# Graph attention and a graph convolution on one core: transposing x1's rows with VectorE and DMA in seven groups of eight, with Strassen products in three more places

## The chip, the cores and the metric

The kernel runs on one core of one Trainium2 chip, in float32 throughout. The metric is the device time of one execution in microseconds. Before the change the median of three runs was 2304.07 us (2303.71 to 2310.33).

## The reference

x is 4096 x 512, adj is 4096 x 4096. Two layers follow one another, each with a residual and a layer norm:

```python
q = x @ Wq.T + bq; k = x @ Wk.T + bk; v = x @ Wv.T + bv
a = q @ k.T / sqrt(512) + adj + adj
x1 = layernorm(x + softmax(a) @ v)
h = relu(adj @ (x1 @ W1) + b1)              # W1: 512 x 128
out = layernorm(x1 + adj @ (h @ W2) + b2)   # W2: 128 x 512
```

## The kernel before

**The arithmetic is rearranged.** With m = the product of Wk and Wq (`psm`, L856), the scores of a group of 512 query rows are x times u, where u = m applied to that group's x, scaled, plus a bias. So there is no q and no k. Behind the softmax, the kernel first forms the exponentials times x (called PX, tile `p`, L576), and only then multiplies the 512 rows of that sum (`ot`) by Wv (`rows_out`, L645, or `rows_out_fast`, L659). Then come the residual, the layer norm, and t = x1 W1 (`project`, `project2`), which layer 1 multiplies by adj.

**Groups and stages.** There are NG = 8 groups of W = 512 query rows. A group's scores (QK, `qk`, L429) are formed in 16 units of seven places; beside the QK products of group g, TensorE runs a paced list of other work: in the first group the u of later groups, afterwards PX of group g - 1, and in it the rows of group g - 2. After the last group's scores there are 16 more units in which PX of group 7 and the rows of group 6 run without QK beside them. Then layer 1 follows (`strassen`, L1049), with the rows of group 7 beside its first block.

**Strassen.** Most products are 2 x 2 block products done in seven multiplications (the Winograd form) rather than eight. `OPERANDS` names the left and right operand of each of the seven, `ORDER` is (1, 2, 6, 7, 5, 4, 3): products 1, 6, 5, 3 accumulate into one PSUM bank (X, or VX, PX) and 2, 7, 4 into others (Y, VY, PY). After each product the bank is read by VectorE (or ScalarE where a result begins) while the next product goes into the other bank; bank X is a single one, so product 1 of the next block of keys has to wait until product 3 has been read. T1 to T4 and S1 to S4 are sums of the blocks, made ahead by VectorE or GpSimd.

**What sets the order.** The schedule is written out by hand: an engine runs its instructions in the order in which the source emits them, and the SP queue issues its DMAs in that order too, each after what it has to wait for. `at(unit, place, f)` hangs a function on a place. `work[unit] = units, items` gives a list of (declared us, function) that is spread evenly over that many units (L1199 to L1219). `row_items` (L754) makes the items of a group's rows; `between`, called `w(n)` in it, takes n products out of the PX list, so that w(4) puts four PX products between two row items.

**The parts that the change touches.**

- Startup (L793 to L879): the four transposed weight halves are loaded, Wq and Wk are transposed by TensorE (`psw`, L848), m is formed (L856), and u of group 0 by plain products (`u_products`, L254, L262); u of group 1 also plainly, in the first three units (`work[0]`). u of groups 2 to 7 is formed by Strassen's products (`u_fast`, L194, L234) in the 13 units after (`work[3]`).
- u's buffers: `new_uo` (L165) has a ring of three for B11 and B12 and one buffer (`uo`, 1280 KB over all partitions) for the other five operands. `store_u` writes them to DRAM (`u_d`), and the group reads them back as `ut` when its turn comes. The large store is issued after product 3.
- Rows: `FAST_V = range(NG - 2)`: rows of groups 0 to 5 by Strassen's products, of 6 and 7 by the plain `rows_out`.
- Projection: `project` (L736) transposes a normalised row tile (128 rows x 512) by four TensorE transposes against the identity into one bank (`x1ps`, L740), ScalarE copies it to `x1t` (L742), and `project2` (L745) multiplies it by W1 (`tps`, L749), after which VectorE copies the 128 x 128 result to `t_sb`. `xr` holds a group's x1 rows; `rowp`, where `xr` and `x1t` lie, has one buffer for each name.
- `add_b2` (L729) adds b2 to a row tile on GpSimd and stores it for the end (`x1_d`).
- `sum_t` (L945): the S sums of t for layer 1, on GpSimd.

Of the kernel before, what the change touches and what calls it, by code (L numbers as in the profile page):

```python
# [11 lines left out]
F32 = mybir.dt.float32  # L12
# [12 lines left out]
def tile_graph_attention_then_gcn(  # L25
# [59 lines left out]
    NCK = N // CW  # L85
    PER = W // P
# [19 lines left out]
    c_d = [dram.tile([1, W], F32, name=f"c_d{g}") for g in range(NG)]  # L106
    u_d = [dram.tile([P, 7, 2, HW], F32, name=f"u_d{g}") for g in range(NG)]
# [46 lines left out]
    FAST_V = range(NG - 2)  # L154
# [10 lines left out]
    def new_uo(b, what):  # L165

        u = UO.setdefault(b, {})
        if what in (B11, B12):
            u[what] = uop.tile([P, 2, HW], F32, tag="b1", name=f"b1_{b}_{what}", bufs=3)
        else:  # L170
            u["all"] = uop.tile([P, 5, 2, HW], F32, tag="ut", name=f"uo{b}")
            u.update({k: u["all"][:, k - 1] for k in range(1, 6)})

    def store_u(b, what):
        if what in (B11, T4):
            nc.gpsimd.dma_start(u_d[b][:, what], UO[b][what])
        else:
            nc.gpsimd.dma_start(u_d[b][:, 1:6], UO[b]["all"])

    def m_sums():  # L180
# [6 lines left out]
        for out_, a, b_ in ((T1, T3, B11), (T2, B22, T1), (T4, B21, T2)):  # L187
            nc.gpsimd.tensor_tensor(MV[out_], MV[a], MV[b_], ALU.subtract)

    def m_t3():  # L190

        nc.vector.tensor_tensor(MV[T3], MV[B22], MV[T3], ALU.subtract)

    def u_fast(b):  # L194
# [4 lines left out]
        def read(k):  # L199
            ps = X["X" if k in (1, 6, 5, 3) else "Y"].rearrange("p (o i) -> p o i", o=2)  # L200
            if k == 1:
                new_uo(b, B11)
            if k == 6:
                new_uo(b, B12)
            if k == 7:
                new_uo(b, "all")
# [10 lines left out]
            if k == 4:  # L217
                for out_, a, b_ in ((T1, B12, B11), (T2, B22, T1), (T3, B22, B12)):
                    nc.gpsimd.tensor_tensor(u[out_], u[a], u[b_], ALU.subtract)
                store_u(b, B11)  # L220
            if k == 3:
                store_u(b, "all")
                owing.append(lambda: last(b))

        def last(b):
            nc.vector.tensor_tensor(UO[b][T4], UO[b][B21], UO[b][T2], ALU.subtract)
            store_u(b, T4)
# [25 lines left out]

    def u_products(b):  # L254

        ps = {}

        def one(o, c):
            def go():
                if c == 0:  # L260
                    ps[o] = bank("o", f"psu{b}_{o}", 4)
                nc.tensor.matmul(  # L262
                    ps[o], m_t[:, c, ts(o, P)], XTS[b][:, c, :], start=c == 0, stop=c == ND - 1
                )
                if c == ND - 1:
                    if o == 0:
                        if b:
                            for what in (B11, B12, "all"):
                                new_uo(b, what)
                        else:  # L270
                            for k in ORDER:
                                new_operand(0, k)
                    pair = (B11, B12) if o < 2 else (B21, B22)
                    for h in range(2):
                        nc.scalar.activation(
                            (UO[b][pair[h]] if b else UT[0, pair[h]])[:, o % 2, :],
                            ps[o][:, ts(h, HW)],
                            AF.Identity,
                            bias=ub_t[:, o : o + 1],
                            scale=HALF_SCALE,  # L280
                        )
                    if o == ND - 1:
                        if b:
                            combine_u(nc.gpsimd, UO[b])
                            for what in (B11, "all", T4):
                                store_u(b, what)
                        else:
# [1109 lines left out]
```

## Time and profile before

| | |
|---|---|
| median of three runs | 2304.07 us (2303.71 to 2310.33) |
| the profiled execution's own time | 2308.84 us |
| its span, first to last instruction | 2307.1 us |
| granted TensorE clock, mean | 0.998 |
| DMA moved | 525.14 MB, mean 228 GB/s |
| transposes of rows (L740) | 128, on TensorE |
| copies of them (L742) | 32 on ScalarE, 587 ns each |
| plain products of u (L262) | 64 pieces, in groups 0 and 1 |
| plain products of rows (L651) | 64 pieces, in groups 6 and 7 |

The page lists an engine's busy time, the chain of work that ended last, the groups of instructions with the idle time before them, and the DMAs with the time from issue to landing. PE is TensorE, PEld its weight loads, DVE is VectorE, ACT is ScalarE, POOL is GpSimd, SP issues DMAs. A float32 matmul of the source stands in the trace as two pieces, a transpose as one. Matmuls are pipelined, so what one costs is the distance from its start to that of its neighbour, not its own duration.

### The profile page before, as it was taken

What the parts mean: (1) busy time and instruction counts of PE and PEld (TensorE: products, weight loads), DVE (VectorE), ACT (ScalarE), POOL (GpSimd) and SP (SyncE); (2) the same over time, 40 slices, a digit from 0 to 9 for tenths busy, and PEclk for the clock granted to TensorE, in tenths of its full rate; (3) what the DMA queues carried; (4) which work ended last, traced back from release to release, by engine and by line L of the source; (5) the groups of instructions that cost most, each with busy time, mean ns of one, the idle gap of its engine ahead of it and who ended that gap; (6) DMA issues with size and microseconds to landing.
All of it is one profiled execution on the core that took longest, in us unless ns stands there. A gap on an engine that the chain in (4) does not pass through costs nothing.

```text
span 2307.1 us, 28475 instructions
## 1 busy us (share of the span) xinstructions
PE 2276.3 (99%) x10672; PEld 1750.6 (76%) x10672; DVE 1617.0 (70%) x2276; ACT 399.8 (17%) x438; POOL 1018.7 (44%) x1009
## 2 busy tenths in 40 slices
PE   9999999999999999999999999999999999999998
PEld 5888788888888888888888888888876743333456
DVE  4676776687667756765776687568657877888864
ACT  2212211131122112111311121122102000000012
POOL 3565654185327424731653274237429830001043
PEclk9999999999999999999999999999999999999999
DMA  6999878667857684777578586947754468899996
GB/s 177 273 284 309 233 215 230 193 174 215 246 135 218 189 246 114 215 213 215 151 221 232 145 218 193 259 117 210 196 191 155 155 237 321 332 347 375 352 383 218
DMA packets 282711, 525.14 MB, mean 228 GB/s; under 512 B 23184, under 2 KB 130448, under 8 KB 281680
## 3 DMA queue, kind: packets, MB, share of 16 engines
q1 hardware_dynamic: 229040, 406.12, 52.3%
q0 software_dynamic: 43296, 105.39, 20.7%
q10 hardware_dynamic: 10240, 11.82, 1.7%
q8 instruction: 85, 1.39, 0.2%
q14 instruction: 50, 0.41, 0.0%
HBM read 475.27 MB, written 46.41 MB: 226 GB/s over the span
## 4 chain that ended last, share of the span: by engine, by line
PE 92%; DVE 4%; POOL 2%; DMA 1%; issue 1%; ACT 0%; SPq 0%; POOLq 0%; DVEq 0%; ACTq 0%
PE p L576 32%; PE X L436 18%; PE b L1041 15%; PE Y L436 14%; PE v L703 3%; PE acce L1342 2%; PE psu L234 2%; PE ops L1296 1%; PE tps L749 1%; PE psu L262 1%; PE x L651 1%; PE x1ps L740 1%; DVE s L449 1%; PE psm L856 1%; DMA u_d<-uo 1%
## 5 line engine op out<-in xcount | busy, mean ns | idle before, releaser
L576 PE MATMUL p<-s,xn 128*128 128x256 f32 x3584 | 895.6, 380 | 7.0 <-DVE s L531 2.6
L576 PEld LDWEIGHTS p<-s,xn 128*128 128x128 f32 x3584 | 677.1, 190 | 111.0 <-DVE s L531 5.6
L436 PE MATMUL X<-ut,sa 128*128 128x256 f32 x1984 | 513.4, 381 | 1.7 <-DVE s L449 1.7
L492 POOL TENSOR_TENSOR lacc<-lacc,s 128x512 f32<-128x512 f32 x240 | 344.1, 1434 | 203.2 <-ACT s L483 192.3
L436 PEld LDWEIGHTS X<-ut,sa 128*128 128x128 f32 x1984 | 370.1, 190 | 64.2 <-DVE s L449 15.3
L449 DVE TENSOR_TENSOR s<-X,s 128x512 f32<-128x512 f32 x256 | 176.3, 689 | 278.6 <-PE X L436 278.2
L436 PE MATMUL Y<-ut,sa 128*128 128x256 f32 x1408 | 361.6, 380 | 0.2 <-DVE s L449 0.2
L436 PEld LDWEIGHTS Y<-ut,sa 128*128 128x128 f32 x1408 | 266.8, 190 | 37.7 <-issue 1.4
L483 ACT ACTIVATE s<-s 128x1024 f32<-128x1024 f32 x128 | 135.3, 1057 | 790.3 <-DVE s L479 790.3
L458 DVE TENSOR_TENSOR macc<-macc,s 128x512 f32<-128x512 f32 x240 | 258.1, 1075 | 1.2
L449 DVE TENSOR_TENSOR s<-Y,s 128x512 f32<-128x512 f32 x192 | 131.9, 687 | 157.0 <-PE Y L436 155.7
L479 DVE TENSOR_TENSOR s<-s,mb 128x512 f32<-128x512 f32 x256 | 231.2, 913 | 2.4 <-ACT mb L399 2.4
L385 POOL DMA_DIRECT2D s<-in_adjT_dram x64 | 84.4, 1318 | 256.7 <-ACT s L380 255.9
L549 DVE TENSOR_TENSOR ot<-p,ot 128x512 f32<-128x512 f32 x248 | 168.9, 681 | 31.4 <-PE p L576 31.2
L1008 DVE TENSOR_TENSOR tt<-ck 128x1024 f32<-128x1024 f32 x112 | 138.4, 1270 | 38.7 <-PE b L1041 33.6
L1041 PE MATMUL b<-tt,st 128*64 128x512 f32 (+1 forms) x768 | 156.0, 541 | 0.0
L380 ACT COPY s<-cb 128x2048 f32<-128x2048 f32 x64 | 121.0, 1890 | 48.1 <-PE p L576 39.8
L519 POOL TENSOR_TENSOR s<-s 128x256 f32<-128x256 f32 x128 | 124.6, 974 | 0.6
L1041 PEld LDWEIGHTS b<-tt,st 128*64 128x64 f32 x768 | 53.9, 137 | 87.8 <-issue 79.9
L526 DVE TENSOR_TENSOR s<-s 128x512 f32<-128x512 f32 x128 | 114.3, 914 | 0.0
L520 POOL TENSOR_TENSOR s<-s 128x256 f32<-128x256 f32 x128 | 107.8, 842 | 10.0
L489 POOL TENSOR_TENSOR lacc<-s 128x512 f32<-128x512 f32 x8 | 10.6, 1321 | 197.9 <-ACT s L483 197.9
(186 smaller groups left out, 2112.6 us busy)
## 6 DMA issues: line engine op xcount, KB each, us to landing
ck<-in_adjT_dram SPq DMA_DIRECT2D x128, 1024.0 KB, 7.4
s<-in_adjT_dram POOLq DMA_DIRECT2D x64, 1024.0 KB, 11.5
sa<-s_d SPq DMA_DIRECT2D x224, 256.0 KB, 5.7
xn<-in_x_dram SPq DMA_DIRECT2D x192, 256.0 KB, 4.3
xn<-xs_d SPq DMA_DIRECT2D x96, 512.0 KB, 5.7
sa<-in_xT_dram SPq DMA_DIRECT2D x168, 256.0 KB, 4.7
xn<-xs_d SPq DMA_DIRECT2D x64, 256.0 KB, 3.9
ut<-u_d SPq DMA_DIRECT2D x49, 256.0 KB, 7.2
```

Source lines behind the costliest of these rows:

```text
L380: nc.scalar.copy(s, CB[g].unsqueeze(1).to_broadcast([P, 4, W]))
L436: nc.tensor.matmul(T["X" if k in (1, 6, 5, 3) else "Y"][:, ts(j, HW)], SA[g, d, a][:, c, j, :], UT[g, b][:, c, :], start=k in (1, 2, 7) an ...
L449: nc.vector.tensor_tensor(ck, ps, ck, ALU.add)
L458: nc.vector.tensor_tensor(MACC[g], MACC[g], ck[:, h, :], ALU.max)
L479: nc.vector.tensor_tensor(ck, ck, MB[g], ALU.subtract)
L483: nc.scalar.activation(ck, ck, AF.Exp, scale=2.0)
L492: nc.gpsimd.tensor_tensor(LACC[g], LACC[g], ck[:, h, :], ALU.add)
L519: nc.gpsimd.tensor_tensor(b12, b12, b11, ALU.subtract)
L549: nc.vector.tensor_tensor(to, ps, to, ALU.add)
L576: nc.tensor.matmul(T["PX" if k in (1, 6, 5, 3) else "PY"][:, ts(f, HW)], XN[n][:, q - a, ts(f, P)], quarters(g, q)[{1: 0, 2: 2, 6: 1, 7: 0 ...
L1008: nc.vector.tensor_tensor(t[:, :2], v[:, :, 1], v[:, 0], ALU.subtract)
L1041: nc.tensor.matmul(BK[n][k][ts(half, HH)], lhs, right(u, i, half, b), start=q == 0, stop=q == NP - 1,)
```

## The change

1. **Transposes of rows.** For groups 0 to 6, `project` is replaced by three steps. `turn_blocks` transposes each 32 x 32 block of the row tile in place of its position with one VectorE instruction, into `x1t`. `store_blocks` writes x1t to DRAM (`xt_d`) with four DMAs of 32 partitions each, issued on SP, so that the blocks land transposed also among each other: each DMA writes 512 runs of 32 elements. `load_blocks` reads the tile back, 128 runs of 2 KB, over the row tile in `xr`, and `project2` multiplies from there. Group 7 keeps `project`.
2. **The order of row items** for those groups is new: b2, turn, store and load of the four row tiles, with w(...) between. `by = 3` (three PX products for one in the last group) is gone, with numbers of its own for group 6.
3. **FAST_V** is `range(NG - 1)`: group 6's rows by Strassen's products too, their operand sums on GpSimd for that group.
4. **u.** `u_products` is gone; u of group 0 by `u_fast` at the startup, its last sums on VectorE, and u of groups 1 to 7 in 15 units from unit 1. B21 joins B11 and B12 in a ring that has four buffers; the single buffer holds the other four operands, and is stored after product 4, not after product 3. B21's store is issued on ScalarE's queue.
5. **Startup.** m's products are taken in another order, beginning before all of Wk has been transposed; m's operand sums are made there, two on VectorE and two on GpSimd, and the first sums of x follow m's second row.
6. **sum_t:** the second half, layer 1's sums over t tiles 16 to 27, is issued three units later.

```diff
+    xt_d = {
+        (g, r): dram.tile([P, ND, P], F32, name=f"xt_d{g}_{r}")
+        for g in FAST_V
+        for r in range(PER)
+    }
...
-    FAST_V = range(NG - 2)
+    FAST_V = range(NG - 1)
...
-        if what in (B11, B12):
-            u[what] = uop.tile([P, 2, HW], F32, tag="b1", name=f"b1_{b}_{what}", bufs=3)
+        if what in (B11, B12, B21):
+            u[what] = uop.tile([P, 2, HW], F32, tag="b1", name=f"b1_{b}_{what}", bufs=4)
         else:
-            u["all"] = uop.tile([P, 5, 2, HW], F32, tag="ut", name=f"uo{b}")
+            u["all"] = uop.tile([P, 4, 2, HW], F32, tag="ut", name=f"uo{b}")
...
     def store_u(b, what):
+        if what == B21:
+            nc.scalar.dma_start(u_d[b][:, what], UO[b][what])
...
             if k == 4:
...
+                if b:
+                    store_u(b, B11)
+                    store_u(b, "all")
             if k == 3:
-                store_u(b, "all")
+                if b:
+                    store_u(b, B21)
...
+        sum_ = (nc.gpsimd if g == NG - 2 else nc.vector).tensor_tensor
...
+    def turn_blocks(g, r):
+        T["x1t", g, r] = rowp.tile([P, ND, P], F32, tag="x1t", name=f"x1t{g}_{r}")
+        nc.vector.transpose(T["x1t", g, r].rearrange("p c i -> p (c i)"), XR[g][:, r, :])
+
+    def store_blocks(g, r):
+        x1t = T.pop(("x1t", g, r))
+        to = xt_d[g, r].rearrange("(b i) c (a j) -> a i c b j", i=32, j=32)
+        for a in range(4):
+            nc.sync.dma_start(
+                to[a], x1t[ts(a, 32)].rearrange("i c (b j) -> i c b j", j=32)
+            )
+
+    def load_blocks(g, r):
+        T["x1t", g, r] = XR[g][:, r, :].rearrange("p (c i) -> p c i", i=P)
+        nc.sync.dma_start(T["x1t", g, r], xt_d[g, r])
...
+            a, b, c, d, e, f = (1, 8, 2, 6, 5, 11) if g < NG - 2 else (3, 14, 4, 10, 6, 22)
             return [
                 *(item(0.86, rows_out_fast, g, k, j) for k in ORDER for j in range(2)),
-                *w(1), item(0, rows_last, g), *norm(2), *norm(3), *w(2), *pro(2), *w(2), *pro(3),
-                *w(1), *norm(0), *w(1), *pro2(2), *norm(1), *w(2), *pro(0), *w(2), *pro2(3), *w(2),
-                *pro(1), *w(2), *pro2(0), *w(4), *pro2(1), *w(2), *b2(2), *w(4), *b2(3), *w(4), *b2(0),
-                *w(4), *b2(1),
+                *w(a), item(0, rows_last, g), *norm(2), *norm(3), *w(b), *norm(0), *w(c), *norm(1),
+                *w(d // 2), *b2(2), *w(d - d // 2), *turn(2), *w(e), *store(2), *b2(3), *w(f),
+                *turn(3), *load(2), *w(e), *store(3), *b2(0), *w(f), *turn(0), *load(3), *pro2(2),
+                *w(e), *store(0), *b2(1), *w(f), *turn(1), *load(0), *pro2(3), *w(e), *store(1),
+                *w(f), *load(1), *pro2(0), *w(f), *pro2(1),
             ]
...
-    work[0] = 3, [(0.86, f) for f in u_products(1)]
-    work[3] = 13, [(0.86, f) for g in range(2, NG) for f in u_fast(g)] + [(0, lambda: owing.pop()())] * 2
-    at(1, 0, m_sums)
-    at(3, 0, m_t3)
+    work[1] = 15, [(0.86, f) for g in range(1, NG) for f in u_fast(g)] + [(0, lambda: owing.pop()())] * 2
...
-            by = 3 if g == NG - 1 else 1
-            items = row_items(g - 1, lambda n: [px.pop() for _ in range(n * by)])
+            items = row_items(g - 1, lambda n: [px.pop() for _ in range(n)])
...
-    at(last_unit - 5, 0, lambda: [sum_t(0, 0, 8), sum_t(8, 8, 14)])
+    at(last_unit - 5, 0, sum_t, 0, 0, 8)
+    at(last_unit - 2, 0, sum_t, 8, 8, 14)
```

## The prediction

> **What bounds the kernel now.** I read the page's busy line first, then its chain, then the groups by form, the chain in order of time, the waits of TensorE, VectorE and the DMA issues.
>
> ```profile
> PE 2276.3 (99%) x10672; PEld 1750.6 (76%) x10672; DVE 1617.0 (70%) x2276; ACT 399.8 (17%) x438; POOL 1018.7 (44%) x1009
> ...
> PE p L576 32%; PE X L436 18%; PE b L1041 15%; PE Y L436 14%; PE v L703 3%; PE acce L1342 2%; PE psu L234 2%; PE ops L1296 1%; PE tps L749 1%; PE psu L262 1%; PE x L651 1%; PE x1ps L740 1%; DVE s L449 1%; PE psm L856 1%; DMA u_d<-uo 1%
> ```
>
> TensorE is busy 99% and nearly the whole chain is matmuls: one microsecond of matmul work less is one microsecond less, unless a wait takes its place. The chain in order of time gives what a piece costs when pieces follow one another (the mean of a group holds the pipeline's depth, so it is too long):
>
> ```profile
> 25.51 3.43 PE psu L262 x8
> 29.38 10.30 PE psu L262 x24
> ...
> 656.18 1.73 PE v L703 x8
> ...
> 870.58 1.73 PE v L703 x8
> ```
>
> A 512-column piece takes 3.43/8 = 0.429 us, a 256-column piece 1.73/8 = 0.216. (Each matmul of the source is two pieces, a transpose one.) The same product returns after 870.58 - 656.18 = 214.4 us: a row group's period. The timeline of TensorE shows a transpose between neighbours:
>
> ```profile
> 893.83 0.66 PE L740 MATMUL x1ps<-ident,xr 128*128 128x128 f32 x4 [0.37 <-ACT xr L639]
> 894.32 0.60 PE L576 MATMUL p<-s,xn 128*128 128x256 f32 x2
> ...
> 896.05 0.60 PE L740 MATMUL x1ps<-ident,xr 128*128 128x128 f32 x4
> 896.49 1.03 PE L436 MATMUL X<-ut,sa 128*128 128x256 f32 x4
> ```
>
> Four transposes hold it 896.49 - 896.05 = 0.44 us, and the first four of a group also wait 0.37 us for the normalised row. TensorE's waits:
>
> ```profile
> PE X L436 <- DVE s L449: 4.1, 5, 1.0
> ...
> PE x1ps L740 <- ACT xr L639: 2.3, 6, 0.4
> PE psu L234 <- ACT uo L211: 1.9, 1, 1.9
> PE x1ps L740 <- ACT x1t L742: 1.5, 1, 1.5
> ...
> PE tps L749 <- ACT x1t L742: 0.7, 1, 0.7
> ```
>
> **The change, part by part.** The profiled execution took 2308.84 us, its span 2307.1.
>
> *Transposes.* Seven groups of four row tiles lose their four PE transposes: 28 x 0.44 = **-12.3 us**. In the changed program's instruction order 16 transposes of rows are left, those of the last group. Their waits go as well: 2.3 for the rows, and 1.5 + 0.7 in the stage where the seventh group's rows are made: **-4.5**. What is late next is project2, which now needs the loaded tile. Its load is issued 16 paced items ahead of it; a list of 113.7 us of declared work (224 products of 0.43, rows 12.0, projections 5.4) is spread over 214.4 us, so an item of 0.43 takes 0.81 us, and 16 take 13 us. The 256 KB loads of xn and sa land in 4 to 6 us, so this stays covered.
>
> *Strassen in three more places.* u of groups 0 and 1 and the rows of group 6 take 28 matmuls of 256 columns in place of 16 of 512: 32 x 0.429 = 13.73 against 56 x 0.216 = 12.10, three times: **-4.9**. Group 0's u is not interleaved with anything; each accumulating bank is read (two ACT pieces of 0.47, or one DVE piece of 0.68) while the other bank takes 1.73 us of product, so I add no wait. The startup's other matmuls are the same ones in another order (the order shows as many of each); DVE reaches c_sb at 22.8 us before, and the new place of the transposes that need it is at about 23.5, so 0.
>
> *u's buffers.* The one big wait of the u stage is 1.9 us for a 1280 KB store of uo that holds the single buffer. Now four of its five parts are stored, a product earlier, and the fifth goes to the ring of four: **-1.9**.
>
> *Group 6's operand sums on POOL.* Three sums precede the sixth product. POOL adds 128x512 in 1.27 to 1.43 us; beginning about 1 us after the last PX read they end at 4.9 to 5.3, and the third product of the order wants the last of them after two products, 3.46 us: **+1.6**. The wait of 0.9 of x (L651) for xr goes with the plain form: **-0.9**.
>
> *VectorE's blocks.* 28 block transposes of 128x512 are not in this trace. Bounds: a copy of that shape 0.69 us, the strided subtraction of L328 1.34 us. I take 0.69 (one input, one output, as the copy), 19 us in all. VectorE's own waits show the cover:
>
> ```profile
> DVE s L449 <- PE X L436: 278.2, 187, 3.2
> DVE s L449 <- PE Y L436: 155.7, 113, 3.2
> ```
>
> It waits for TensorE 434 us, 1.5 at a time, and the bank it empties is needed again one product later (1.73 of its own, 2.0 of the interleaved list), so it may be about 2.5 us late before PE waits. Only where product 3 is followed by product 1 in the same bank is there no slack; the 4.1 us above are those. 28 transposes of 0.69, one product in seven: at most 28 x 0.69 / 7 = 2.8, **+1.5** taken; without cover it is 19 to 37.
>
> *The trip through DRAM, the real unknown.* x1t has one buffer, so the next tile's block transpose (VectorE, in order) waits until all four stores of the tile before have landed, and behind it queue the reads of X, Y and p that TensorE waits for. SP's load of the tile waits for the same landings, and behind it queue the sa and xn loads; those are issued some five products ahead, 19 us, and need 6, so SP can stand about 13 us and VectorE gives way first. Stores and transpose are 11 items apart, 8.9 us (22 items of 0.43, 9.5 us, in group 6). Each store writes 512 runs of 128 bytes. The nearest rows:
>
> ```profile
> c_d<-c_sb ACTq DMA_DIRECT2D x7, 2.0 KB, 9.8
> ...
> s_d<-sa SPq DMA_DIRECT2D x32, 256.0 KB, 7.8
> x_d<-xb POOLq DMA_DIRECT2D x32, 256.0 KB, 4.0
> ```
>
> c_d's store is 512 runs too, of 4 bytes; s_d's are four stores in a row on SP. Low end: 256 KB lands as x_d, 4.0. High end: the four follow one another at c_d's pace, 39. I take 9, between s_d (four issues) and c_d (short runs): as long as the window, so VectorE is held little and its 2.5 us of slack take most of it. 21 such waits (three a group): **+2** for the queueing of some behind large loads.
>
> The Trainium skill, page "DMA: Bandwidth & Descriptors", section "Rules for kernel authors", speaks against this step: a transpose by rearranged access pattern in a plain DMA is put at 19 times the hardware's, and its "Specifications" ask for 512 bytes or more a run. c_d's 9.8 us for 2 KB agrees in direction; no run here shows 128 bytes. An estimate from the page alone: 256 KB at its 435 GB/s is 0.6 us, 19 times that 11.4, on top of s_d's 7.8 gives 19 us, 10 past the window, and 21 x (10 - 2.5) = +160 us. I weigh it less, because runs of 32 elements are not single elements.
>
> *Moves.* The later second sum_t and the spread row items in the last two stages, and the ACT copies saved, hide behind other work: 0.
>
> Sum: -12.3 - 4.5 - 4.9 - 1.9 + 1.6 - 0.9 + 1.5 + 2 = -19.4. On the profiled execution's own time: 2308.8 - 19.4 = 2289.4. The median of the runs is 4.8 under that execution (2304.07), so **2284.6**; I say 2285.
>
> **Rivals.**
> (a) *The stores hold VectorE.* One mechanism: four stores land late, the next block transpose stands at the head of VectorE, X and Y are not read. Each microsecond past 8.9 + 2.5 = 11.4 costs 21. Without the +2 the gain is 21.4, so it turns the sign at 11.4 + 1.0 = 12.4 us. At 15 us: 21 x 3.6 - 21.4 = +54, 2358; at c_d's pace (39 us) 21 x 27.6 = 580 more, 2860. For it: c_d's short runs. Against: the x_d and s_d rows with far more bytes.
> (b) *Half the gain goes in the last stage.* From 1700 to 1860 us TensorE already waits for VectorE and POOL (L531, L526, L549: 5.2 us) and the change adds seven reads of 0.68 for four, and four block transposes. At 5 to 10 us more: 2290 to 2295.
> (c) *That stage gets better.* Row items stood between 96 products, now 165, so VectorE's bursts are thinner; if the 5.2 us and as much of their smaller kin go: 2275.
> (d) *Waits of 1 us at each of the 21 places* beyond the +2: no change, 2304.
>
> **Chances.** Forecast 0.56, (b) 0.15, (c) 0.12, (d) 0.04, (a) 0.13. About 0.3%, 7 us, is what a measurement here tells from no change. Faster: 0.56 + 0.15 + 0.12 = 0.83; same 0.04; slower 0.13. The range reaches from 2266 (case (c), low ends of the unknowns) to 2303, leaving out (a), some of (d) and little below.
>
> **What would show it.** Right: no x1ps in groups 0 to 6, PE busy down by about 18, sixteen plain row matmuls left of 32, block transposes near 0.7 us, stores landing in under 11 us, no new TensorE wait over 5 us. Wrong: a line "DVE x1t <- DMA" of tens of microseconds, with waits of X and Y on s behind it; loads of sa or xn late on SP; or block transposes well over 1.3 us.

## The result, and the profile after

The changed kernel takes **2325.2 us** (median, 2323.64 to 2329.25), the kernel before in the same comparison 2305.07: **ratio 1.0086, 95% interval 1.0073 to 1.0099**. It is slower by about 20 us, where 2285 was forecast. The profiled execution's span grew from 2307.1 to 2327.4 us.

The busy line and the chain of the page after:

```profile
PE 2267.3 (97%) x10632; PEld 1753.7 (75%) x10632; DVE 1636.9 (70%) x2315; ACT 386.3 (17%) x414; POOL 1024.6 (44%) x1007
...
PE p L550 30%; PE X L410 18%; PE b L1054 15%; PE Y L410 13%; PE v L679 3%; PE psu L252 3%; PE acce L1356 2%; DVE s L453 2%; PE ops L1310 1%; PE tps L743 1%; DVE s L500 1%; DVE s L505 1%; DVE s L423 1%; DMA t_sb<-in_x_dram 1%; DVE macc L432 1%
```

TensorE has 40 pieces fewer, as counted out (112 transposes less, three times 56 for 32 more), and is busy 9 us less, but its share fell from 99% to 97%, and five lines of VectorE stand in the chain in place of one. TensorE's longest sums of waits in the kernel after (total, times, longest, us):

```profile
PE p L550 <- DVE ot L523: 21.1, 14, 1.7
PE p L550 <- DVE s L500: 8.7, 14, 1.7
PE X L410 <- DVE s L423: 6.7, 4, 4.7
PE p L550 <- DVE s L505: 4.1, 7, 0.6
```

L550 is the PX product (L576 before), L523 its read, L500 and L505 the sums of exponentials that are its operands. The same three waits before:

```profile
PE p L576 <- DVE s L531: 2.6, 2, 1.7
PE p L576 <- DVE s L526: 2.3, 5, 0.7
PE p L576 <- DVE ot L549: 1.4, 2, 0.9
```

What was feared did not come: the block transposes and their stores, in the kernel after:

```profile
L725 DVE STREAM_TRANSPOSE x1t<-xr x28: 694/699/703, 477.8 to 1816.5; 128x512 f32<-128x512 f32 x28
```

```profile
DMA to landing us min/median/max: 2.2/4.9/11.7
```

0.70 us each, never lengthened, and VectorE has no wait on x1t's stores at all.

**Where the time came.** By the first matmul of each stage: the startup is 1.4 us shorter, the stages of groups 0 and 1 (the u work) together 1.7 longer, the six stages in which rows of groups 0 to 5 are made **21.0 longer**, the stage after the last scores 1.4 shorter, layer 1 the same 368.7, the tail 0.4 longer: +20.3. The six are alike, so one is enough. In the stage of group 3's scores I mark three points: the first PX product, the 57th (the end of the stretch in which the first 56 products stand beside the rows' other work; the *short stretch* below) and the last (the *long stretch*). Busy time by stretch, before; the columns are window, its length, then busy us and instructions of PE, PEld, DVE, ACT and POOL, clock, DMA share and GB/s:

```profile
676.70:732.80 56.10, 55.67 (x277) 48.09 (x277) 45.74 (x63) 18.32 (x21) 46.89 (x47) 1.00 0.69 189
732.80:867.20 134.40, 134.40 (x625) 117.33 (x624) 85.81 (x120) 19.35 (x16) 48.95 (x42) 1.00 0.80 223
```

The same two stretches after:

```profile
681.00:734.40 53.40, 48.47 (x222) 40.52 (x221) 46.52 (x58) 13.07 (x15) 48.02 (x46) 1.00 0.81 207
734.40:874.70 140.30, 140.30 (x665) 123.13 (x664) 87.64 (x129) 22.20 (x18) 49.35 (x43) 1.00 0.84 225
```

The reader is to see two things. The short stretch lost 55 TensorE pieces and is only 2.7 us shorter; TensorE now stands idle in it for 5 us, with VectorE busy 46.5 and GpSimd 48.0 of 53.4 us. The long stretch gained 40 pieces and is 5.9 us longer, TensorE busy without a gap in both kernels. Two queries of the same windows tell which pieces went over. Those of the scores (L436), before:

```profile
676.70:732.80 56.10, 30.02 (x117) 1.00 0.69 189
732.80:867.20 134.40, 72.44 (x281) 1.00 0.80 223
```

and of the scores (L410) after:

```profile
681.00:734.40 53.40, 25.90 (x101) 1.00 0.81 207
734.40:874.70 140.30, 76.44 (x297) 1.00 0.84 225
```

Sixteen score pieces changed sides, and the projections of three tiles too (32 pieces of `tps` stood in the short stretch before, 8 stand there after, 24 in the long one).

### The profile page after: what moved, and what is told of

The parts are those of the page before. It is cut to its first block, busy times and chain, and to the rows that moved or that the text cites. A ratio compares the mean times of both kernels' runs of the same rounds, so it can differ in the third digit from the quotient of the medians.

```text
span 2327.4 us, 28683 instructions
## 1 busy us (share of the span) xinstructions
PE 2267.3 (97%) x10632; PEld 1753.7 (75%) x10632; DVE 1636.9 (70%) x2315; ACT 386.3 (17%) x414; POOL 1024.6 (44%) x1007
## 4 chain that ended last, share of the span: by engine, by line
PE 88%; DVE 7%; DMA 3%; issue 1%; SPq 0%; POOL 0%; ACT 0%; POOLq 0%; DVEq 0%
PE p L550 30%; PE X L410 18%; PE b L1054 15%; PE Y L410 13%; PE v L679 3%; PE psu L252 3%; PE acce L1356 2%; DVE s L453 2%; PE ops L1310 1%; PE tps L743 1%; DVE s L500 1%; DVE s L505 1%; DVE s L423 1%; DMA t_sb<-in_x_dram 1%; DVE macc L432 1%
## 5 line engine op out<-in xcount | busy, mean ns | idle before, releaser
L550 PE MATMUL p<-s,xn 128*128 128x256 f32 x3584 | 899.1, 381 | 35.6 <-DVE ot L523 21.1
L550 PEld LDWEIGHTS p<-s,xn 128*128 128x128 f32 x3584 | 677.2, 190 | 148.4 <-DVE ot L523 26.7
L410 PE MATMUL X<-ut,sa 128*128 128x256 f32 x1984 | 514.3, 382 | 5.8 <-DVE s L423 5.8
L410 PEld LDWEIGHTS X<-ut,sa 128*128 128x128 f32 x1984 | 372.2, 190 | 68.3 <-DVE s L423 20.3
L410 PE MATMUL Y<-ut,sa 128*128 128x256 f32 x1408 | 360.6, 379 | 2.4 <-DMA sa<-in_xT_dram 2.4
L410 PEld LDWEIGHTS Y<-ut,sa 128*128 128x128 f32 x1408 | 266.0, 190 | 38.1 <-DVE s L453 2.7
L453 DVE TENSOR_TENSOR s<-s,mb 128x512 f32<-128x512 f32 x256 | 237.0, 932 | 0.4 <-ACT mb L373 0.4
L432 DVE TENSOR_TENSOR macc<-macc,s 128x512 f32<-128x512 f32 x240 | 227.8, 949 | 1.4
L523 DVE TENSOR_TENSOR ot<-p,ot 128x512 f32<-128x512 f32 x248 | 168.9, 681 | 27.1 <-PE p L550 27.0
L1021 DVE TENSOR_TENSOR tt<-ck 128x1024 f32<-128x1024 f32 x112 | 138.9, 1275 | 38.7 <-PE b L1054 34.1
L500 DVE TENSOR_TENSOR s<-s 128x512 f32<-128x512 f32 x128 | 126.3, 1007 | 0.0
L493 POOL TENSOR_TENSOR s<-s 128x256 f32<-128x256 f32 x128 | 123.3, 963 | 0.6
L494 POOL TENSOR_TENSOR s<-s 128x256 f32<-128x256 f32 x128 | 118.1, 923 | 10.1
L463 POOL TENSOR_TENSOR lacc<-s 128x512 f32<-128x512 f32 x8 | 10.6, 1322 | 199.0 <-ACT s L457 199.0
## 6 DMA issues: line engine op xcount, KB each, us to landing
s<-in_adjT_dram POOLq DMA_DIRECT2D x64, 1024.0 KB, 11.7
```

What stands on the lines that cost most here:

```text
L410: nc.tensor.matmul(T["X" if k in (1, 6, 5, 3) else "Y"][:, ts(j, HW)], SA[g, d, a][:, c, j, :], UT[g, b][:, c, :], start=k in (1, 2, 7) an ...
L432: nc.vector.tensor_tensor(MACC[g], MACC[g], ck[:, h, :], ALU.max)
L453: nc.vector.tensor_tensor(ck, ck, MB[g], ALU.subtract)
L493: nc.gpsimd.tensor_tensor(b12, b12, b11, ALU.subtract)
L500: nc.vector.tensor_tensor(b, b, t2, ALU.subtract)
L523: nc.vector.tensor_tensor(to, ps, to, ALU.add)
```

## The experiments

Times are medians; ratios are against the kernel before, run beside them, with their 95% intervals. Stretch lengths are those of a middle group.

**1. Which part of the change?** The rows of groups 0 to 5 alone put back, all else changed:

```diff
+            if g < NG - 2:
+                return [
...
+                    *w(1), item(0, rows_last, g), *norm(2), *norm(3), *w(2), *pro(2), *w(2), *pro(3),
...
             a, b, c, d, e, f = (1, 8, 2, 6, 5, 11) if g < NG - 2 else (3, 14, 4, 10, 6, 22)
```

> The changed kernel with the rows of groups 0 to 5 made as before the change (TensorE transposes, old order of row items); group 6, u and the startup stay changed. After the change each of the six row stages is 3.3 to 3.9 us longer than before, the startup 1.4 and u 0.5 shorter, the last stage 1.5 shorter. All theories put the loss into the rows of groups 0 to 5, so all expect about 2300 us (2297 to 2304). Above 2312 would mean that the loss lies elsewhere.

Measured 2304.38, ratio 0.9991 (0.998 to 1.0002). So the loss lies in those rows. The rest of the change together is worth about 2 us, by the interval between 4.6 us gained and 0.5 lost.

**2. The trip.** No stores and no loads:

```diff
-        for a in range(4):
-            nc.sync.dma_start(
-                to[a], x1t[ts(a, 32)].rearrange("i c (b j) -> i c b j", j=32)
-            )
...
-        nc.sync.dma_start(T["x1t", g, r], xt_d[g, r])
```

> The changed kernel without the stores to DRAM and the loads back (it leaves out the trip, so project2 multiplies the untransposed tile); block transposes, b2 and the order of items stay. Trip theory (short runs hold VectorE, SP or the DMA engines): the six stages lose their 5.5 us each, about 2292. Beside theory (b2 on GpSimd and block transposes on VectorE fall into the stretch in which VectorE has the short PX blocks): 2318 to 2326. Pace theory (the PX list runs earlier against the shifts because no projection holds it back): 2318 to 2326.

Measured 2324.36, 1.0077 (1.0062 to 1.0092): the trip costs nothing here.

**3. VectorE's transposes.** Left out, the stores reading the row tile:

```diff
-        T["x1t", g, r] = rowp.tile([P, ND, P], F32, tag="x1t", name=f"x1t{g}_{r}")
-        nc.vector.transpose(T["x1t", g, r].rearrange("p c i -> p (c i)"), XR[g][:, r, :])
+        T["x1t", g, r] = XR[g][:, r, :].rearrange("p (c i) -> p c i", i=P)
```

> The changed kernel without the 28 block transposes (the stores read the row tile itself; it leaves out the transposes inside the blocks); trip, b2 and order stay. Balance theory: in the first 56 PX products of a group (the short blocks) VectorE needs about 11 us for 14 products, as long as TensorE, so what is added to VectorE there is waited for by TensorE: three of a group's four block transposes fall there, 2 to 3 us a group less, 2307 to 2314. If VectorE had cover there (the step of the prediction: 2.8 us in all): 2321 to 2325.

Measured 2326.76, 1.0094 (1.0079 to 1.0109). The theory of a balance of VectorE's time fell in this form: 0.70 us less of VectorE at each of the 28 tiles gave nothing.

**4. Later, and slower.** All row items behind the first two norms later (`b` from 8 to 64), and a declared weight for the turns:

```diff
-            a, b, c, d, e, f = (1, 8, 2, 6, 5, 11) if g < NG - 2 else (3, 14, 4, 10, 6, 22)
+            a, b, c, d, e, f = (1, 64, 2, 6, 5, 11) if g < NG - 2 else (3, 14, 4, 10, 6, 22)
```

> The changed kernel with one number changed: 64 PX products in place of 8 before norm of the third row tile in groups 0 to 5, so that b2, block transposes and trips come behind the short PX blocks. Beside theory: the VectorE waits at about 70 to 80 us into a group go, about 2293 (2290 to 2300). Pace theory: the short blocks come as early as before this edit, the waits stay, 2318 to 2326. Trip theory: the trips are all there, 2320 to 2326.

```diff
-                lambda r, f=f: [item(0, f, g, r)] for f in (turn_blocks, store_blocks, load_blocks)
+                lambda r, f=f: [item(1.34 if f is turn_blocks else 0, f, g, r)] for f in (turn_blocks, store_blocks, load_blocks)
```

> The changed kernel with a declared 1.34 us on each block transpose item, as project and project2 together had, so that the PX list is held back as if the projections were still there; all else stays. Pace theory: the waits of the six stages go, 2293 to 2300. Beside theory: b2 and turns still fall into the short blocks, 2315 to 2326. Trip theory: 2320 to 2326.

The later one took 2316.89, 1.0047 (1.0032 to 1.0062): short stretch 48.5, long 143.7, and a time that none of its three theories had. The one with a declared weight took 2337.75, 1.0129 (1.0111 to 1.0146): 56.5 and 138.6, above every range. A declared weight does no TensorE work; it only brings 12 more score pieces into the short stretch, and those bring their own reads for VectorE and sums for GpSimd.

**5. Is TensorE the bound in the short stretch?** Four idle transposes at each turn, as many as the change had taken away:

```diff
     def turn_blocks(g, r):
...
+        ps = mbank(f"idle{g}_{r}")
+        for c in range(ND):
+            nc.tensor.transpose(ps[:, ts(c, P)], XR[g][:, r, ts(c, P)], ident)
...
-                lambda r, f=f: [item(0, f, g, r)] for f in (turn_blocks, store_blocks, load_blocks)
+                lambda r, f=f: [item(0.44 if f is turn_blocks else 0, f, g, r)] for f in (turn_blocks, store_blocks, load_blocks)
```

> The changed kernel with four idle TensorE transposes of the row tile beside each block transpose (their result is read by nobody): 28 x 0.44 = 12.3 us more work for TensorE. Balance theory: three of four fall where TensorE waits for VectorE anyway, so that most of it is free: 2323 to 2331. If TensorE's work sets the time throughout (the prediction's premise): 2337.

Measured 2326.07, 1.009 (1.0075 to 1.0105): the 12.3 us of TensorE work that the prediction counted as the gain can be put back without cost. The declared 0.44 us moves no scores here: 101 score pieces stand in the short stretch, as in the kernel after. Three of a group's four turns fall into the short stretch, which takes 52.6 us with them (53.4 in the kernel after), the fourth into the long one, which takes 140.9 (140.3).

**6. GpSimd's share.** b2 left out in groups 0 to 5, added by VectorE, added twice:

```diff
+        if g < NG - 2:
+            nc.gpsimd.dma_start(x1_d[i // 2][:, i % 2], XR[g][:, r, :])
+            return
...
```

> The changed kernel without the addition of b2 on GpSimd in groups 0 to 5 (the rows are stored as they are; it leaves out that sum); turns and trips stay. In the traces a VectorE operation with two SBUF operands takes 0.68 us alone and 1.3 to 1.4 beside GpSimd. If b2 beside the short blocks slows VectorE in this way: 1 to 3 us a group less, 2307 to 2319. If not: 2323 to 2326.

```diff
-        nc.gpsimd.tensor_tensor(xb, XR[g][:, r, :], b2_t, ALU.add)
+        (nc.vector if g < NG - 2 else nc.gpsimd).tensor_tensor(xb, XR[g][:, r, :], b2_t, ALU.add)
```

> The changed kernel, with the four b2 additions of a row group (groups 0 to 5) on VectorE in place of GpSimd; everything else stands where it stood. Theory (in the 56 PX products behind the rows GpSimd is the late engine, VectorE partly behind it): 2305 to 2316, because VectorE adds such a tile in 0.68 us when GpSimd is idle against 1.3 to 1.8 on GpSimd. Rival (the sum of VectorE's and GpSimd's time counts, or what hurts is the store of x1 itself and its buffer): 2320 to 2330.

```diff
-        nc.gpsimd.tensor_tensor(xb, XR[g][:, r, :], b2_t, ALU.add)
+        for _ in range(2 if g < NG - 2 else 1):
+            nc.gpsimd.tensor_tensor(xb, XR[g][:, r, :], b2_t, ALU.add)
```

> The changed kernel, with GpSimd's b2 addition done twice for each row tile of groups 0 to 5 (24 more additions, 31 to 43 us of GpSimd's time in all). Theory (GpSimd sets the pace there): 2337 to 2345, about as much lost as leaving the additions out won (16.6 us). Rival (GpSimd has slack, leaving b2 out helped by something else, such as the order of its DMA): 2324 to 2329.

Without b2: 2308.61, 1.0018 (1.0006 to 1.003), short stretch 50.2. On VectorE: 2319.87, 1.0061 (1.0043 to 1.008), 52.2. Twice: 2332.58, 1.0119 (1.0104 to 1.0134), 54.5 in most groups, at a granted clock of 0.97 in five of the six and of 1.00 in one, which is as long. The long stretch is 140.3 in all three. So these additions do set the pace there, with the sign of the theory in all three, but twice of them costs 7 us where none of them wins 17, and both the VectorE version and the doubled one lie between theory and rival. That both engines count, and not GpSimd alone, is the reading that fits; what follows shows one way.

How the two can hold each other is seen in the timeline of the kernel after, VectorE and then GpSimd, with start and duration in us:

```profile
721.36 1.75 DVE L453 TENSOR_TENSOR s<-s,mb 128x512 f32<-128x512 f32 x1
723.03 1.76 DVE L432 TENSOR_TENSOR macc<-macc,s 128x512 f32<-128x512 f32 x1
724.71 0.68 DVE L523 TENSOR_TENSOR ot<-p,ot 128x512 f32<-128x512 f32 x1
```

```profile
721.08 3.15 POOL L466 TENSOR_TENSOR lacc<-lacc,s 128x512 f32<-128x512 f32 x2 [0.84 <-ACT s L457]
```

L453 has a median of 0.68 us; beside GpSimd's two additions it and L432 take 1.75 and 1.76, and the read of p, one of whose inputs lies in PSUM, begins some 2.2 us later for it but is not longer itself. TensorE's next product stood 1.43 us for that read. The Trainium skill, page "SBUF — State Buffer", section "Who interferes with whom", says that a VectorE instruction with two SBUF inputs contends with a GpSimd instruction that reads SBUF, the later one standing until the other is done; the rows agree. The block transposes (one input, 0.694 to 0.703 us in all 28, 22 of them for more than half of their time beside a GpSimd addition) agree with its other half, that an instruction with one SBUF input, outside the modes that use two ports, does not.

**7. The additions moved to layer 1.** Rows stored without b2 from ScalarE's queue, GpSimd adding b2 when the x1 pairs are loaded:

```diff
-        nc.gpsimd.tensor_tensor(xb, XR[g][:, r, :], b2_t, ALU.add)
...
-        nc.gpsimd.dma_start(x1_d[i // 2][:, i % 2], xb)
+        nc.scalar.dma_start(x1_d[i // 2][:, i % 2], XR[g][:, r, :])
...
+                    nc.gpsimd.tensor_tensor(
+                        XP[n], XP[n], b2_l.unsqueeze(1).to_broadcast([P, 2, D]), ALU.add
+                    )
```

> The changed kernel, with b2 not added in the rows at all: the x1 rows are stored as they are, from ScalarE's queue, and GpSimd adds b2 in layer 1, when a pair of x1 tiles has been loaded for the end. Same output. Theory (GpSimd's b2 additions beside the short blocks are the loss): 2303 to 2310, as without b2 (2308.6). Rival (the loss is only moved: GpSimd's additions in the tail of layer 1 are waited for there): 2312 to 2325.

Measured 2313.39, 1.003 (1.0017 to 1.0043), as the rival had it. The short stretches are 50.2 as without b2, but the tail has a new wait of TensorE:

```profile
PE ops L1313 <- DVE xp L1315: 5.3, 3, 2.6
```

**8. Two tiles by TensorE, two by the trip.** First with the trips in the long stretch, then again with b2 in layer 1:

```diff
...
+                    *w(1), item(0, rows_last, g), *norm(2), *norm(3), *w(2), *pro(2), *w(2), *pro(3),
+                    *w(1), *norm(0), *w(1), *pro2(2), *norm(1), *w(4), *pro2(3), *w(60), *b2(2),
+                    *w(5), *b2(3), *w(5), *b2(0), *w(4), *turn(0), *w(5), *store(0), *b2(1), *w(11),
+                    *turn(1), *load(0), *w(5), *store(1), *w(11), *load(1), *pro2(0), *w(11), *pro2(1),
```

> Groups 0 to 5: two row tiles projected with TensorE transposes in the short blocks, as before the change, and two by block transposes and the trip in the long blocks behind, b2 there too. Balance theory: TensorE work in the short blocks is covered by VectorE, turns in the long blocks by TensorE; a group's stage is 1 us shorter than with all four by TensorE (213.9), about 2298 (2295 to 2302). If turns cost wherever they are: 2304 to 2312.

```diff
...
+                    *w(1), item(0, rows_last, g), *norm(2), *norm(3), *b2(2), *b2(3), *w(2), *pro(2),
+                    *w(2), *pro(3), *w(1), *norm(0), *b2(0), *w(1), *pro2(2), *norm(1), *b2(1), *w(4),
+                    *pro2(3), *w(4), *turn(0), *w(5), *store(0), *w(16), *turn(1), *load(0), *w(5),
+                    *store(1), *w(16), *load(1), *pro2(0), *w(16), *pro2(1),
```

> b2 in layer 1 as in the run before the last, and in groups 0 to 5 two of the four row tiles transposed by TensorE right behind the rows as before the change, the other two by VectorE and DMA, 16 PX products between a store and what follows it. Theory (in the short blocks TensorE's transposes are free, in the long blocks each is worth its 0.44 us; GpSimd relieved): 2294 to 2303, better than both kernels. Rival (VectorE's transposes are held by stores in the long blocks and delay the banks, as in the earlier two-and-two kernel): 2306 to 2318.

Both missed the theory: 2320.1, 1.0063 (1.0048 to 1.0078), above its other range too, and 2317.43, 1.0048 (1.0033 to 1.0063). In the first, the prediction's rival (a) appears; VectorE's waits have this line:

```profile
DVE x1t L725 <- DMA xt_d<-x1t: 21.8, 5, 6.0
```

The second lies in its rival's range, but the rival's wait is gone from it (16 products between the steps); short and long stretch are 52.2 and 139.1, and TensorE waits 4.8 us in the tail, where it waited 5.3 in 7. With two projections still in the long stretch these do not tell the theories well apart.

**9. The place of TensorE's work.** What 4 to 8 had not touched is the long stretch: 140.3 us wherever b2 went. So one kernel moves only the projections of groups 0 to 5 back into the short stretch (they multiply the row tile as it stands, so the transposition is left out of what they use, while turn, stores and loads all run), and another makes the move in the kernel before, with no trip at all:

```diff
     def project2(g, r):
-        x1t = T.pop(("x1t", g, r))
+        if g < NG - 2:
+            x1t = XR[g][:, r, :].rearrange("p (c i) -> p c i", i=P)
...
+                    *w(1), item(0, rows_last, g), *norm(2), *norm(3), *w(8), *norm(0), *pro2(2), *w(2), *norm(1),
+                    *w(2), *pro2(3), *w(1), *b2(2), *w(3), *pro2(0), *turn(2), *w(5), *store(2), *pro2(1), *b2(3), *w(11),
+                    *turn(3), *load(2), *w(5), *store(3), *b2(0), *w(11), *turn(0), *load(3),
+                    *w(5), *store(0), *b2(1), *w(11), *turn(1), *load(0), *w(5), *store(1), *w(11), *load(1),
```

> The changed kernel with its trip as it stands, but the projections of groups 0 to 5 moved back into the first 56 PX products; to be free of the trip they multiply the row tile as it stands (the transposition is left out of what they use, not of the work done). Theory (TensorE work moved from the stretch that VectorE and GpSimd bound to the one that TensorE bounds): the long stretch of a group back from 140.3 to about 134.5, the short one from 53.4 to 53.5 to 55, in all 2290 to 2303. Rival (the b2 sums and their collisions alone): 2320 to 2330.

```diff
-                *w(1), item(0, rows_last, g), *norm(2), *norm(3), *w(2), *pro(2), *w(2), *pro(3),
...
+                *w(1), item(0, rows_last, g), *norm(2), *norm(3), *w(5), *norm(0), *w(1), *norm(1),
+                *w(16), *b2(2), *w(4), *b2(3), *w(4), *b2(0), *w(4), *b2(1), *w(28), *pro(2), *w(2), *pro(3),
+                *w(2), *pro2(2), *w(2), *pro(0), *w(2), *pro2(3), *w(2), *pro(1), *w(2), *pro2(0), *w(4), *pro2(1),
```

> The kernel before, with nothing changed but the place of the transposes and projections of groups 0 to 5: behind the 56th PX product in place of inside the first 35. Theory: the short stretch falls from 55.7 to 51 to 54 only, the long one rises from 134.4 to 141 to 143, so 2322 to 2340, without any block transpose or DMA trip. Rival (TensorE's work counts the same wherever it stands, as the prediction took it): 2303 to 2309.

Both came as the theory had them. Projections early: **2298.17, 0.997 (0.9958 to 0.9982)**, 27 us less than the changed kernel. Its two stretches:

```profile
679.10:731.90 52.80, 52.02 (x254) 45.06 (x253) 47.16 (x64) 13.79 (x16) 48.14 (x46) 1.00 0.79 204
731.90:867.70 135.80, 135.80 (x632) 118.85 (x631) 84.67 (x123) 21.70 (x18) 48.71 (x42) 1.00 0.86 235
```

The kernel before with its projections late: **2330.58, 1.011 (1.0094 to 1.0126)**, 25 us more, without a block transpose or a trip. Its stretches:

```profile
677.50:726.80 49.30, 45.38 (x205) 38.27 (x204) 43.95 (x52) 13.07 (x15) 45.39 (x45) 1.00 0.76 203
726.80:871.70 144.90, 144.90 (x697) 127.01 (x696) 89.44 (x130) 24.44 (x22) 50.82 (x44) 1.00 0.77 211
```

In the first TensorE is busy 52.0 of 52.8 us: its work has come back into the cover, and the short stretch did not grow for it (53.4 in the changed kernel). In the second the short stretch fell by 6.8 us for some 10.5 of work taken out, and the long one rose by the whole 10.5. All four kernels by the same count of pieces (0.216 us for one of 256 columns; a projection's piece is taken from the two long stretches, (140.3 - 135.9 - 8 x 0.216)/24 = 0.11; a transpose is the 0.11 that the prediction measured; eight small pieces of each long stretch count 0.3 together):

| | short: TensorE's work | short: length | long: TensorE's work | long: length |
|---|---|---|---|---|
| before | 54.6 | 55.6 to 56.1 | 133.1 | 134.4 |
| after | 46.7 | 53.4 | 139.2 | 140.3 |
| projections early | 51.1 | 52.8 | 134.8 | 135.9 |
| before, projections late | 44.1 | 49.4 | 143.6 | 144.9 |

The long stretch is TensorE's work plus 1.1 to 1.3 us in every row (for the second and third row partly by construction, since the 0.11 comes from them). The short one is TensorE's work plus 1.0 to 1.7 us in the two rows with 51 us of work or more; in the other two it is 6.7 and 5.3 us above it. There is no fixed floor: with the declared weight of experiment 4 the short stretch took 56.5 us for 49.3 of work.

**10. b2 later in the kernel before.** If GpSimd bounded the short stretch in any order, moving b2 out of it would win in the kernel before as well:

```diff
-                *pro(1), *w(2), *pro2(0), *w(4), *pro2(1), *w(2), *b2(2), *w(4), *b2(3), *w(4), *b2(0),
+                *pro(1), *w(2), *pro2(0), *w(4), *pro2(1), *w(43), *b2(2), *w(4), *b2(3), *w(4), *b2(0),
```

> The kernel before, with the four b2 additions of groups 0 to 5 moved from products 23 to 35 to products 64 to 76, where GpSimd is half idle. Theory (before the change the short stretch, 55.7 us with 54.5 us of TensorE work, is bound by TensorE): 2299 to 2305, at most 1.2 us a group. Rival (GpSimd's b2 bounds that stretch in any order): 2285 to 2293, the 16.6 us that leaving b2 out won after the change.

Measured 2316.07, 1.0045 (1.003 to 1.0061). In the short stretch it went as the theory had it: GpSimd's busy time fell from 46.9 to 38.7 us, and the length only from 56.1 to 55.5. The total missed for another reason. In the long stretch GpSimd's additions now meet VectorE's, whose busy time rose from 85.8 to 91.9, and TensorE, which had no wait there before, waits for VectorE's reads of the scores:

```profile
731.00:867.20 136.20, 135.08 (x624) 117.01 (x623) 91.86 (x120) 19.35 (x16) 57.79 (x50) 1.00 0.81 224
```

```profile
PE X L436 <- DVE s L449: 1.1, 2, 0.6
```

That is 1.1 of the 1.8 us by which the stretch grew. GpSimd was busy 49 of 134 us there before, and still there was no room for it.

**11. A trip with its projections inside the stretch.** Three versions: trips ten products apart, the same with the turned tiles in the ring of eight buffers of `sa`, and two tiles by TensorE with the other two by the trip early:

```diff
...
+                    *w(1), item(0, rows_last, g), *norm(2), *norm(3), *w(3), *turn(2), *w(2), *b2(2), *w(1),
+                    *store(2), *w(1), *norm(0), *w(2), *norm(1), *w(4), *turn(3), *w(1), *b2(3), *w(1), *load(2),
...
+                    *w(8), *load(1), *w(2), *pro2(0), *w(8), *pro2(1),
```

> The changed kernel, computing the same, with the trips of groups 0 to 5 set closer (about 10 PX products from one tile's transpose to the next and from a load to its projection), so that all four projections stand within the first 56 PX products. Theory: as the run before, 2292 to 2305, better than both kernels if nothing else waits. Rival (the stores then hold VectorE's next transpose, or the projection waits for its load): 2310 to 2330, with a wait of VectorE for x1t's store or of TensorE for the load.

```diff
+        if g < NG - 2:
+            T["x1t", g, r] = sap.tile([P, ND, P], F32, tag="sa", name=f"x1t{g}_{r}")
...
```

> The tight trip, computing the same, with the turned tiles of groups 0 to 5 in the ring of eight buffers that also serves sa and xb, in place of the single x1t. Theory (the single buffer made VectorE wait for the stores, and that wait alone took the gain back): 2293 to 2305. Rival (the stores themselves, four issues of up to 4.1 us each on SP, hold the loads of xn and sa and the loads of the turned tiles, whatever the buffer): 2315 to 2350.

```diff
...
+                    *w(1), item(0, rows_last, g), *norm(2), *norm(3), *w(2), *pro(2), *w(2), *pro(3),
+                    *w(1), *norm(0), *w(1), *pro2(2), *norm(1), *w(4), *pro2(3), *w(2), *turn(0), *w(3), *b2(2),
...
+                    *w(1), *b2(1), *w(4), *pro2(0), *w(5), *load(1), *w(11), *pro2(1),
```

> The changed kernel, computing the same, with two row tiles of groups 0 to 5 transposed by TensorE right behind the rows, the other two by VectorE and DMA from the 13th product on, single buffer, and all four projections inside the short stretch. Theory (place of TensorE's work decides, few stores in flight do no harm): long stretch 136 us, short one 53 to 55, in all 2295 to 2305. Rival (a trip inside the short stretch holds VectorE or SP there at any spacing): 2310 to 2330.

Measured 2354.23, 1.0208 (1.019 to 1.0226); 2372.34, 1.0291 (1.0275 to 1.0306); 2335.48, 1.0128 (1.0111 to 1.0145): all three above both of their ranges. The long stretch is 135.9, 135.9 and 135.5 as the theory has it, but the short one 62.1 to 66.7 in the first two and about 59 in the third. The granted clock in the short stretches was 0.95 to 0.97 in the first and 0.90 to 0.92 in the second (1.00 in the kernel after), so a part of their length may be the clock's; no run tells how much. In the first, VectorE waits for x1t's stores:

```profile
DVE x1t L725 <- DMA xt_d<-x1t: 28.1, 10, 5.0
```

With the ring that wait is gone, and VectorE waits instead for a tile of the ring, 34.2 us in five waits that the trace puts down to GpSimd and 6.6 in a sixth. In all six the transposition begins 0.08 us after the landing of a store of a b2 tile, and b2's tiles use the same ring. In the third, SP's queue stands at the load of a turned tile, which overwrites the row tile that b2 is still to read:

```profile
SPq L737 <- POOL xb L708: 57.6, 6, 10.1
```

So set closely, the trip hangs on its own stores in the first and on GpSimd's late b2 in the other two. None of the kernels that do the whole work beat the kernel before by more than the noise (the old rows of experiment 1 come closest, at 0.9991). A close trip with b2 in layer 1 was not tried.

## Why the prediction was wrong

**The step that failed** is the first one: "TensorE is busy 99% and nearly the whole chain is matmuls: one microsecond of matmul work less is one microsecond less, unless a wait takes its place". Nor has the sum any term for the projections of groups 0 to 5, which the new order puts behind the trip; its paragraph on moves, "hide behind other work: 0", speaks of the last two stages. The share of 99% was right for the span and wrong as a price, because the schedule has two stretches with two limits. In the short one TensorE's transposes and projections were cover for VectorE and GpSimd; in the long one each piece costs its full 0.216 or 0.11 us. The change took 1.8 us of transposes and three projections out of the first and put the projections into the second; and since the list is spread by declared time, 16 score pieces followed them. Per group that is 16 x 0.216 + 24 x 0.11 = 6.1 us to pay in the long stretch (5.9 measured), while of 7.9 us less in the short one only 2.2 to 3.2 came back, and waits of TensorE for VectorE (4.9 us in the stretch shown) took the place of the rest: +3.3 on average, six times, and 0.2 a group ahead of them: the 21.0 us.

It could have been worked out. The list's 113.7 us was in the prediction, used only for a window, and a group's scores are 448 pieces in the trace (3584 in eight groups): 1.76 + 2.7 us of declared work leaving the early part move 4.46 x 448/113.7 = 17.6 pieces (16 measured). And busy time by stretch showed GpSimd at 46.9 and VectorE at 45.7 us beside 54.6 of TensorE's work, 46.7 of which would be left.

Its other steps:

- *Transposes, -12.3, and their waits.* The pieces went as counted, and idle ones of the same size could be put back for nothing (experiment 5). Of the forecast for the six row stages, -10.6 - 2.3 + 1.5 + 2 = -9.4, +21.0 came: 30 of the 40 us between forecast and result.
- *u and startup, -3.3 and -1.9.* +0.3 came: the startup won 1.4, the first two score stages lost 1.7. A new wait of 4.7 us stands there for a read by VectorE (third line of the waits above), and VectorE waited 16.5 us for x's rows in t_sb where it had waited 9.7. The timeline shows that the one caused the other: VectorE stands 8.91 us for the rows, reads the bank right behind them, and TensorE goes on after that.

```profile
150.26 0.69 DVE L382 SCALAR_TENSOR_TENSOR t_sb<-t_sb,g_t 128x512 f32<-128x512 f32 x1 [8.91 <-DMA t_sb<-in_x_dram]
150.88 0.69 DVE L423 TENSOR_TENSOR s<-X,s 128x512 f32<-128x512 f32 x1
```

```profile
151.62 1.22 PE L410 MATMUL X<-ut,sa 128*128 128x256 f32 x2 [4.69 <-DVE s L423]
```

- *The last stage*, about -4.9 by its terms: -1.4. The wait for the POOL sums was 1.2 where 1.6 was taken.
- *Block transposes, 0.69 each, +1.5*: 0.70, and no cost (experiment 3).
- *The trip, 9 us taken, +2*: 4.9 for one store at the median, 11.7 at most. The 9 us were for a tile's four stores together; from the first one's issue to the last one's landing they took 4.2 to 12.6, 7.0 at the median. There was no cost at this spacing (experiment 2): the next block transpose began 1.8 us or more after the landing. The estimate of 19 us, worked out from the factor of 19 that the Trainium skill gives in "DMA: Bandwidth & Descriptors", section "Rules for kernel authors", does not hold for these runs of 128 bytes. The factor itself compares with the hardware's transposing DMA, which no run here used.
- *Rivals.* None named the cause. (a) was the slower case, and its mechanism is real: it shows where the steps stand closer (8, 11), not in this change. A slower result came by another road.
- *Signs.* Those listed as "right" came for the pieces and for the block transposes; the longest landing of a store passed 11 us by little. Two did not: TensorE's busy time fell by 9 us, not 18, and new waits appeared, 21.1 and 8.7 us in sum, in pieces of at most 1.7.

**Still open**: why the length to which the short stretch falls differs (50.2 without b2, 49.4 in the kernel before with late projections, 53.4 after, 56.5 with the declared weight). Order and the meetings of the two engines matter, and no run separates them.

## What to carry to other kernels

A share of 99% over the span does not price a microsecond of the bounding engine; take busy time by stretch, and ask in each what the other engines need without it. Where a list is paced by declared costs, work out what else slides when an item leaves. Before counting on work saved, put idle work of the same size where it stood, or move the same work in the old kernel: either tells at once whether that place pays.

## What the runs showed of the hardware

- In the kernel after, VectorE's 128x512 addition with both inputs in SBUF (L453) takes 0.68 us at the median where GpSimd adds nothing at the time, and 1.21 at the median of the 107 instances that lie for more than half of their time beside GpSimd's additions (1.75 in the rows above). The same operation with one input in PSUM (L523) takes 0.68 in both cases, and 32 x 32 block transposes of that shape take 0.70.
- Four stores of 512 runs of 128 bytes, 64 KB each, landed in 4.9 us each at the median (2.2 to 11.7); x1's stores of 256 KB in long runs took 4.4 at the median in the same execution.
